# A gate stage as one hand-ordered stream over rows of 8x8 blocks, in a four-layer convolution and scan kernel

## The chip, the cores and the metric

The kernel runs on one core of one Trainium2 chip. The metric is the device time of one execution in microseconds; where several executions are compared, their median is given. All arithmetic is float32.

## The reference, cut to what matters

An image batch x of shape (2, 128, 128, 128) (two images, 128 channels, 128 by 128 pixels) goes through four layers. Layers 0 and 2 are a 3x3 convolution, a small selective scan (mamba) of 8 tokens per pixel, a group norm, a SiLU and a residual. Layer 3 is a residual block of two 3x3 convolutions with batch norm. Layer 1, which the change concerns, weighs x with a gate made from local densities:

```python
g = x.reshape(B, GROUP, c, hh, WINDOW, ww, WINDOW)      # 4 groups of 32 channels, 16 x 16 windows of 8 x 8
g = g.transpose(0, 1, 3, 5, 2, 4, 6).reshape(B * GROUP * hh * ww, c, WINDOW * WINDOW)
sq = jnp.sum(g * g, axis=-1)
gram = jnp.einsum('ncw,ndw->ncd', g, g)
dist2 = jnp.maximum(sq[:, :, None] + sq[:, None, :] - 2.0 * gram, 0.0)
K = jnp.exp(-0.5 * dist2 / (BW * BW))
density = K.mean(axis=-1)                                # one number per channel and window
y = jnp.einsum('bchw,oc->bohw', density, w1) + b1[None, :, None, None]
y = jax.nn.relu(y)
y = jnp.einsum('bchw,oc->bohw', y, w2) + b2[None, :, None, None]
attn = jax.nn.sigmoid(y) + GAMMA                         # GAMMA = 0.5
attn = upsample_bilinear_ac(attn, WINDOW)                # 16 x 16 -> 128 x 128, corners aligned
return x * attn
```

The norm, SiLU and residual of layer 0 need statistics over a whole image, so the kernel computes them in the gate stage too, just ahead of the densities.

## The kernel before, in words

The program runs in five parts, one after another: mamba layer 0 (`_mamba`, lines 296 to 580), the gate stage (`_gates`, 602 to 775), mamba layer 2 (the same function again), the norms, and the residual block (`_basic_block`). Each part opens its own buffer pools and closes them at its end, so a part's first buffers come free when the part before has let go of that memory. A tile framework gives out buffers and sets every semaphore. It also lets two engines touch the same PSUM bank only one after the other, even when both only read. Within `_mamba` the order of each engine's instructions is written out by hand (`tc.manual_schedule`, line 577). In `_gates` of the kernel before it is not: there the framework's scheduler orders each engine's queue by the order of the program text and by what is ready.

Work in `_gates` goes by rows of windows: a row is (b, y0), image b and one of 16 rows of 8x8 windows, 8 pixel rows high, so 128 channels by 1024 pixels. There are 32 rows. For each row:

- `load` (629) brings the mamba output (tile g) and the layer's input (tile xr) from memory, 512 KB each; ScalarE applies the norm and SiLU to g (636), GpSimd adds xr and stores the sum by windows in a tile x (638).
- `turn` (646) transposes x in eight pieces of 128x128 on TensorE into a PSUM tile pt (652). VectorE copies pt out as xt (654) and ScalarE squares it into xq (656). ScalarE also squares x itself into sq (659), VectorE sums that for each window (661) and scales the sums by -0.5 (662): nsq.
- `density` (665) makes the Gram matrices on TensorE: 8 matmuls with the constant -0.5 (671) and 64 of 32x32 (681), in eight tiles of the array side by side. VectorE adds nsq out of PSUM (689, tile kk), GpSimd clips at 0 (695), ScalarE takes the Exp (696).
- `total` (699) sums kk over channels on VectorE into dens (700).

When the 16 rows of an image have their densities, `gain` (702) computes the gates of the whole image: one matmul with w1, a Relu, and for each of four groups of windows two matmuls (717, 718), a Sigmoid (719) and an addition of 0.5 (720). From then on `apply` (722) is called once in each step of the loop: it upsamples one row of the gates on TensorE (738), in matmuls that contract 32 partitions (two neighbouring gate rows), and multiplies it into x on VectorE (747), in one to two pieces a row; ScalarE's queue issues the store (751). So the loop (756 to 773) runs image 0's densities alone, then image 1's densities with image 0's upsampling, and the last line (775) runs image 1's upsampling alone. All 16 rows of an image wait in SBUF for their gates (tile x has nh + 5 = 21 buffers). Large PSUM tiles (pt, the upsampled rows, the gates) share one tag with two buffers of three banks.

ScalarE's functions come in tables: Silu has one, Exp another, Sigmoid a third, and an instruction that changes the table (a table load) stands in ScalarE's queue wherever the next function needs another one. Square and Relu need no change.

Of the kernel before, what the change touches and what calls it, by code (L numbers as in the profile page):

```python
# [24 lines left out]
F32 = mybir.dt.float32  # L25
U8 = mybir.dt.uint8
AF = mybir.ActivationFunctionType
ALU = mybir.AluOpType
AX = mybir.AxisListType
PSUM = bass.MemoryType.PSUM  # L30

P = 128
# [7 lines left out]
WIN = 8  # L40
# [37 lines left out]
def _bilinear(n):  # L78

    m = n // WIN  # L80
    at = np.arange(n, dtype=np.float32) * np.float32((m - 1) / (n - 1))
    i0 = np.clip(np.floor(at).astype(np.int32), 0, m - 2)
    return i0, (at - i0.astype(np.float32)).astype(np.float32)
# [8 lines left out]
def _place(k):  # L92


    q = k // 2
    return k % 2 + 2 * (q // 4), q % 4


def _upsampling(H):

    _, fy = _bilinear(H)
    ix, fx = _bilinear(P)
    wx = np.zeros((P // WIN, P), np.float32)
    wx[ix, np.arange(P)] = 1.0 - fx
    wx[ix + 1, np.arange(P)] += fx
    segs = _segments(H)
    up = np.zeros((4, 2, P // WIN, 4, max(e - a for _, a, e in segs), P), np.float32)
    for k, a, e in segs:
        n, g = _place(k)
        for h in range(a, e):  # L110
            up[g, 0, :, n, h - a] = (1.0 - fy[h]) * wx
            up[g, 1, :, n, h - a] = fy[h] * wx
    return up.reshape(P, 4, -1)
# [488 lines left out]
def _gates(tc, src, w, con, y, stats, wm, b1, up, dst, H):  # L602

    nc = tc.nc
# [3 lines left out]
    nwin = nh * nw  # L608
    segs = _segments(H)
    with tc.tile_pool(name="dg", bufs=2) as dp, tc.tile_pool(name="dg1", bufs=1) as sp, tc.tile_pool(  # L610
        name="ps_t", bufs=2, space=PSUM
    ) as pst, tc.tile_pool(name="ps_g", bufs=1, space=PSUM) as psg:

        def wide():
            return pst.tile([P, 3 * ROWS, P], F32, tag="pt", name="pt")

        class Small:


            def tile(self, shape, dtype, tag=None, name=None):  # L620
                return wide().rearrange("p a b -> p (a b)")[: shape[0], : shape[1]]

        norm = [_norm(nc, sp, Small(), w, con, stats, b) for b in range(B)]
        ct = sp.tile([P, 4, up.shape[2]], F32, tag="ct", name="ct")

        dens = [sp.tile([P, nh, 2, npair], F32, tag=f"dens{b}", name="dens") for b in range(B)]
        held, live, gains = {}, {}, {}

        def load(b, y0):

            rows = slice(y0 * WIN, (y0 + 1) * WIN)
            g = dp.tile([P, WIN, P], F32, tag="g", name="g", bufs=4)
            nc.sync.dma_start(out=g, in_=y[b][:, rows, :])
            xr = dp.tile([P, WIN, P], F32, tag="xr", name="xr", bufs=4)
            nc.sync.dma_start(out=xr, in_=src[b][:, rows, :])
            nc.scalar.activation(g, g, AF.Silu, bias=norm[b][1], scale=norm[b][0])
            x = held[b, y0] = dp.tile([P, nw, WIN, WIN], F32, tag="x1", name="x1", bufs=nh + 5)
            nc.gpsimd.tensor_tensor(by_row(x), by_row(xr, False), by_row(g, False), ALU.add)
# [6 lines left out]

        def turn(b, y0):

            x = held[b, y0].rearrange("p x r w -> p (x r w)")

            pt = wide()[:, :npair, :]  # L650
            for k in range(npair):
                nc.tensor.transpose(pt[:, k, :], x[:, k * P : (k + 1) * P], con["ident"])
            xt = dp.tile([P, npair, P], F32, tag="xt", name="xt")
            nc.vector.tensor_copy(xt, pt)
            xq = dp.tile([P, npair, P], F32, tag="xq", name="xq")
            nc.scalar.activation(xq, pt, AF.Square)

            sq = dp.tile([P, nw, WIN * WIN], F32, tag="sq", name="sq", bufs=1)
            nc.scalar.activation(sq.rearrange("p x r -> p (x r)"), x, AF.Square)
            nsq = dp.tile([P, nw], F32, tag="nsq", name="nsq")  # L660
            nc.vector.tensor_reduce(nsq, sq, AX.X, ALU.add)
            nc.vector.tensor_scalar_mul(nsq, nsq, -0.5)
            live[b, y0] = xt, xq, nsq

        def density(b, y0):
            xt, xq, nsq = live.pop((b, y0))
# [21 lines left out]
            kk = dp.tile([P, 2, npair, CG], F32, tag="kk", name="kk", bufs=3)  # L688
# [8 lines left out]
            live[b, y0] = kk  # L697

        def total(b, y0):
            nc.vector.tensor_reduce(dens[b][:, y0], live.pop((b, y0)), AX.X, ALU.add)  # L700

        def gain(b):

            den = sp.tile([P, nh, npair, 2], F32, tag="den", name="den")
            nc.vector.tensor_scalar_mul(den, dens[b].rearrange("p y a k -> p y k a"), 1.0 / CG)
            p1 = wide().rearrange("p a b -> p (a b)")[:CG, :nwin]
            nc.tensor.matmul(p1, lhsT=wm["w1"], rhs=den.rearrange("p y k a -> p (y k a)"), start=True, stop=True)
            hid = sp.tile([CG, nwin], F32, tag="hid", name="hid")
            nc.scalar.activation(hid, p1, AF.Relu, bias=b1)
            p2 = wide()[:, :4, :]  # L710
            gt = gains[b] = sp.tile([P, 4, P], F32, tag="gain", name="gain")
            for n in range(4):
                at = (n % 2 + n // 2 * WIN) * nw
                m = min(P, nwin - at) // 32 * 32
                if m <= 0:
                    continue
                nc.tensor.matmul(p2[:m, n, :], lhsT=hid[:, at : at + m], rhs=wm["w2"], start=True, stop=False)
                nc.tensor.matmul(p2[:m, n, :], lhsT=wm["one"][:, :m], rhs=wm["b2"], start=False, stop=True)
                nc.scalar.activation(gt[:m, n, :], p2[:m, n, :], AF.Sigmoid)
                nc.vector.tensor_scalar_add(gt[:m, n, :], gt[:m, n, :], 0.5)  # L720

        def apply(b, y0):

            r0 = y0 * WIN
            pu = wide()
            o = dp.tile([P, WIN, P], F32, tag="g", name="o", bufs=4)
            x = by_row(held.pop((b, y0)))

            cut = [a for k, a, _ in segs if k % 2 == 0 and r0 < a < r0 + WIN]
            at = 0  # L730
            for first, end in zip([r0, *cut], [*cut, r0 + WIN]):
                for r in range(first, end, ROWS):
                    for k, a, e in segs:
                        lo, hi = max(a, r), min(e, r + ROWS, end)
                        if lo < hi:
                            n, g = _place(k)
                            q = slice(g * 32, (g + 1) * 32)
                            nc.tensor.matmul(
                                pu[:, at + lo - first : at + hi - first, :],
                                lhsT=gains[b][q, n, :],  # L740
                                rhs=ct[q, n, (lo - a) * P : (hi - a) * P],
                                start=True,
                                stop=True,
                                tile_position=(q.start, 0),
                            )
                rows = slice(first - r0, end - r0)
                nc.vector.tensor_tensor(
                    by_row(o[:, rows, :], False), by_row(pu[:, at : at + end - first, :], False), x[:, rows], ALU.mult
                )
                at += (end - first + ROWS - 1) // ROWS * ROWS  # L750
            nc.scalar.dma_start(out=dst[b][:, r0 : r0 + WIN, :], in_=o)

        order = [(b, y0) for b in range(B) for y0 in range(nh)]
        N = len(order)
        ready = []
        for n in range(-4, N + 2):
            if ready:
                apply(*ready.pop(0))
            if n % 2 == 0:
                for i in range(n + 4, min(n + 6, N)):  # L760
                    load(*order[i])
            if n == -4:
                nc.sync.dma_start(out=ct, in_=up)
            if 0 <= n < N:
                turn(*order[n])
            if 1 <= n <= N:
                density(*order[n - 1])
            if n >= 2:
                b, y0 = order[n - 2]
                total(b, y0)  # L770
                if y0 == nh - 1:
                    gain(b)
                    ready += [(b, i) for i in range(nh)]
        for at in ready:
            apply(*at)
# [141 lines left out]
def _program(ctx, tc, d, cols, out):  # L917
# [7 lines left out]
    with tc.tile_pool(name="const", bufs=1) as cp, tc.tile_pool(name="wts", bufs=1) as wp:  # L925
# [6 lines left out]
        w2 = cp.tile([CG, 3, P], F32, tag="w2", name="w2")  # L932
# [3 lines left out]
        wm = {"w1": w1, "w2": w2[:, 0, :], "b2": w2[:, 1, :], "one": w2[:, 2, :]}  # L936
# [18 lines left out]
def _host_layout(inputs):  # L955
# [9 lines left out]
    w2b = np.zeros((CG, 3, P), np.float32)  # L965
    w2b[:, 0] = np.asarray(inputs["L1_conv_w2"]).T
    w2b[0, 1] = np.asarray(inputs["L1_conv_b2"])
    w2b[:, 2] = 1.0
# [27 lines left out]
```

## Time and profile before

| | |
|---|---|
| time, median of 3 executions | 7872.17 us (7866.06 to 7881.12) |
| profiled execution | 7862.75 us; span of the core 7860.9 us |
| granted TensorE clock, mean over the span | 0.923 of full |
| busy share of the span | PE 83%, DVE 87%, ACT 55%, POOL 70% |
| last multiply of the gate stage (L747) ends | about 3633.6 us from the start |
| first load of the next layer's rows can start | 3638.4 us |

The profile's short names are: PE for TensorE's matmuls and PEld for its weight loads, DVE for VectorE, ACT for ScalarE, POOL for GpSimd, SP for the queue that issues most transfers. L652 is line 652 of the kernel. In the tables of stretches, each engine's busy time in microseconds stands with its number of instructions in brackets; after the engines come the granted clock, the busy share of the transfer engines and GB/s. In the timeline, each line is a start and a duration in microseconds, engine, line, operation, and tiles (out<-in); what stands in square brackets at the end is the idle time of the engine before the instruction, and what ended it.

A float32 matmul shows as two records on TensorE, a transpose as one.

### The profile page before, as it was taken

How to read it: one execution, taken by the hardware profiler on the slowest of the kernel's cores; microseconds unless marked ns; L12 is line 12 of the kernel's file. 1: busy time of each engine (PE TensorE's matmuls, PEld its weight loads, DVE VectorE, ACT ScalarE, POOL GpSimd, SP SyncE). 2: the span in 40 equal slices, each digit the busy share in tenths (PEclk: the TensorE clock that was granted, in tenths of full speed). 3: DMA queues.
4: the chain of work that ended last, by engine and by line, in shares of the span. 5: the costliest groups of instructions: out<-in, count | busy, mean ns of one | idle time of the engine just before them, and what ended most of it. 6: DMA issues, size and time to landing. Idle time of an engine off the chain costs nothing. (4 is left out here: it accounts for less than half of the span.)

```text
span 7860.9 us, 86792 instructions
## 1 busy us (share of the span) xinstructions
PE 6537.9 (83%) x29412; PEld 2217.4 (28%) x29412; DVE 6831.1 (87%) x6360; ACT 4291.8 (55%) x4835; POOL 5521.1 (70%) x1810
## 2 busy tenths in 40 slices
PE   7888888888888888777888888888888888878893
PEld 2222222222222222253222222222222222223341
DVE  5999999999999999863999999999999999963454
ACT  5656666666666656482665665666656656621112
POOL 5777887777778777652777778787777777843330
PEclk8999999999999999866999999999999999979996
DMA  7999999999999999854999999999999999955204
GB/s 203 246 243 246 253 249 247 253 250 256 249 248 254 245 249 248 225 179 127 244 249 246 250 250 251 252 251 253 252 239 249 250 250 250 250 157 139 69 0 163
DMA packets 573435, 1765.42 MB, mean 225 GB/s; under 512 B 85536, under 2 KB 239680, under 8 KB 458176
## 3 DMA queue, kind: packets, MB, share of 16 engines
q1 hardware_dynamic: 530496, 1709.54, 84.0%
q10 hardware_dynamic: 42496, 50.34, 1.8%
q8 instruction: 234, 3.83, 0.2%
q14 instruction: 209, 1.71, 0.1%
HBM read 1549.82 MB, written 209.72 MB: 224 GB/s over the span
## 5 line engine op out<-in xcount | busy, mean ns | idle before, releaser
L451 POOL TENSOR_TENSOR h<-ur,bcr 128x2048 f32<-128x2048 f32 x896 | 4060.4, 4539 | 1193.2 <-DMA bcr<-sb 1006.0
L478 DVE TENSOR_TENSOR set<-set,h 128x1024 f32<-128x1024 f32 x1792 | 2193.0, 1224 | 301.6 <-ACT set L469 216.2
L479 DVE TENSOR_TENSOR r<-set,bcr 128x1024 f32<-128x1024 f32 x1792 | 2194.1, 1224 | 61.4
L469 ACT ACTIVATE set<-set 128x1024 f32<-128x1024 f32 x1792 | 1745.6, 1006 | 868.7 <-PE set L460 854.2
L483 DVE TENSOR_TENSOR h<-set,h 128x1024 f32<-128x1024 f32 x1536 | 1864.5, 1214 | 21.3 <-POOL h L451 21.2
L460 PE MATMUL set<-dt,rep 32*128 32x512 f32 x7168 | 1400.2, 674 | 96.8 <-DVE h L483 89.9
L498 PE MATMUL ys<-r,ct 128*32 128x512 f32 x7168 | 1166.1, 632 | 36.4 <-DVE r L479 36.0
L328 PE MATMUL one<-band,conv 128*128 128x512 f32 x2304 | 1085.5, 607 | 24.6 <-DMA band<-in_x_dram 12.2
L828 PE MATMUL m<-comb,u 128*128 128x512 f32 x1536 | 689.1, 610 | 88.5 <-DVE Y L842 53.2
L406 PE MATMUL one<-xc,keep 128*64 128x512 f32 x1024 | 324.6, 717 | 471.4 <-ACT xc L363 361.5
L460 PEld LDWEIGHTS set<-dt,rep 32*128 32x128 f32 x7168 | 405.2, 193 | 992.7 <-issue 466.2
L328 PEld LDWEIGHTS one<-band,conv 128*128 128x128 f32 x2304 | 408.2, 190 | 674.4 <-issue 599.2
L489 PE MATMUL ys<-t,ct 128*128 128x512 f32 x512 | 326.4, 724 | 252.4 <-DVE v L511 250.9
L357 ACT ACTIVATE xc<-one,keep 128x512 f32<-128x512 f32 x256 | 176.1, 688 | 519.5 <-PE one L355 514.7
L498 PEld LDWEIGHTS ys<-r,ct 128*32 128x32 f32 x7168 | 181.2, 111 | 928.5 <-issue 760.7
L828 PEld LDWEIGHTS m<-comb,u 128*128 128x128 f32 x1536 | 296.6, 195 | 480.3 <-issue 457.3
L426 PE MATMUL one<-prod,ct 128*128 128x512 f32 x512 | 290.3, 650 | 123.1 <-POOL prod L418 88.8
L380 POOL TENSOR_TENSOR u<-dt,xc 128x1024 f32<-128x1024 f32 x128 | 302.8, 2366 | 70.7 <-ACT dt L374 70.6
L355 PE MATMUL one<-y,w_in 128*128 128x512 f32 x512 | 343.5, 759 | 5.8 <-ACT xc L357 3.1
L469 ACT ACT_TABLE_LOAD x252 | 323.3, 1283 | 4.6
L370 PE MATMUL one<-xc,w_dt 128*128 128x512 f32 x512 | 313.5, 696 | 4.1 <-ACT bc L413 4.1
L427 ACT COPY t<-one 128x512 f32<-128x512 f32 x256 | 150.2, 587 | 301.4 <-PE one L426 301.4
(136 smaller groups left out, 5894.0 us busy)
## 6 DMA issues: line engine op xcount, KB each, us to landing
ur<-su SPq DMA_DIRECT2D x896, 896.0 KB, 11.5
bcr<-sb SPq DMA_DIRECT2D x896, 448.0 KB, 11.6
ur<-su SPq DMA_DIRECT2D x896, 128.0 KB, 11.1
su<-u SPq DMA_DIRECT2D x1024, 64.0 KB, 3.5
sb<-bc SPq DMA_DIRECT2D x256, 224.0 KB, 2.8
bcr<-sb SPq DMA_DIRECT2D x896, 64.0 KB, 10.9
y<-o SPq DMA_DIRECT2D x128, 256.0 KB, 9.2
band<-in_x_dram SPq DMA_DIRECT2D x28, 640.0 KB, 10.9
```

The source lines that it names most:

```text
L328: nc.tensor.matmul(py.rearrange("p (r w) -> p r w", r=ROWS), lhsT=w["conv"][:, tap, :], rhs=xb[:, r + kh : r + kh + ROWS, kw : kw + P], st ...
L355: nc.tensor.matmul(p, lhsT=w[("in", "z")[i]][:, g, :], rhs=s["y"], start=True, stop=True)
L406: nc.tensor.matmul(p[g * NQ * DS : (g + 1) * NQ * DS, :], lhsT=w[("xb", "xcm")[i]], rhs=s["xc"][:, g, :], start=True, stop=True,)
L451: nc.gpsimd.tensor_tensor(b, s["ur", t], s["bc", t][:, 0].unsqueeze(1).to_broadcast([P, NJ, NS]), ALU.mult)
L460: nc.tensor.matmul(a[j // 2][:, j % 2, :], lhsT=w["rep"][r, q, :], rhs=s["dt"][r, g, :], start=True, stop=True, tile_position=(r.start, 0),)
L469: nc.scalar.activation(x, x, AF.Exp)
L478: nc.vector.tensor_tensor(pt, pt, s["h", t - 1][:, js, :], ALU.mult)
L479: nc.vector.tensor_tensor(s["r", t][:, js, :], pt, s["bc", t - 1][:, 1].unsqueeze(1).to_broadcast([P, 2, NS]), ALU.mult)
L483: nc.vector.tensor_tensor(s["h", t][:, js, :], pt, s["h", t][:, js, :], ALU.add)
L489: nc.tensor.matmul(s["ys", g], lhsT=con["ident"], rhs=s["t1"][:, g, :], start=True, stop=False)
L498: nc.tensor.matmul(s["ys", g][a : a + NQ * DJ, :], lhsT=red[:, q, :], rhs=r[:, j, :], start=False, stop=(q == NQ - 1), tile_position=(0, a),)
L828: nc.tensor.matmul(m[:, i], lhsT=u[:, i, kw, :], rhs=v[:, i, :, kw : kw + P], start=(kw == 0), stop=(kw == 2),)
```

## The change

The stage becomes one stream over all 32 rows. Each row's gate is made as soon as the densities of its neighbours are there, instead of once for an image, and is used five to seven steps after the row's densities were begun. So a row of x waits for its gate in one of 14 buffers instead of 21, the upsampling of both images runs beside densities, and the order of every engine's queue is written out: step n of the loop runs the stages of rows n, n-1, n-2, n-3, n-5, n-6 and n-7, in the order in which the list `stages` has them. The Sigmoid is computed as 1 / (1 + exp(-y)), with ScalarE's Exp and a reciprocal on VectorE, so the stage needs two tables, and rows are loaded and their Silu is applied in pairs, on even steps. The upsampling contracts 64 partitions (four gate rows, of which the weights use up to three), with two matmuls of 512 columns for each row of windows. The stores are issued from SP's queue.

The diff, cut to its core:

```diff
+    up = np.zeros((2, 4, P // WIN, H // WIN, ROWS, P), np.float32)
+    for h in range(H):
+        y0, r = divmod(h, WIN)
+        for y, f in ((iy[h], 1.0 - fy[h]), (iy[h] + 1, fy[h])):
+            if f != 0:
+                up[r // ROWS, y - y0 + 1, :, y0, r % ROWS] = f * wx
...
-        def wide():
-            return pst.tile([P, 3 * ROWS, P], F32, tag="pt", name="pt")
...
+        weights = sp.tile([P, nh, ROWS * P], F32, tag="up", name="up")
+        nc.sync.dma_start(out=weights.rearrange("p y n -> p (y n)"), in_=up)
+        hidden = []
+        for b in range(B):
+            h = sp.tile([CG, nh + 3, nw], F32, tag=f"hid{b}", name="hid")
+            nc.gpsimd.memset(h, 0.0)
+            hidden.append(h)
...
+        def residual(b, y0):
+            s = live[b, y0]
+            g, xr = s.pop("g"), s.pop("xr")
+            nc.scalar.activation(g, g, AF.Silu, bias=norm[b][1], scale=norm[b][0])
+            s["x"] = dp.tile([P, nw, WIN, WIN], F32, tag="x1", name="x1", bufs=14)
+            nc.gpsimd.tensor_tensor(by_row(s["x"]), by_row(xr, False), by_row(g, False), ALU.add)
...
         def turn(b, y0):
-            pt = wide()[:, :npair, :]
+            pt = pst.tile([P, npair, P], F32, tag="pt", name="pt")
...
-        def gain(b):
-            den = sp.tile([P, nh, npair, 2], F32, tag="den", name="den")
...
-                nc.scalar.activation(gt[:m, n, :], p2[:m, n, :], AF.Sigmoid)
-                nc.vector.tensor_scalar_add(gt[:m, n, :], gt[:m, n, :], 0.5)
+        def hide(b, y0):
+            p = psg.tile([CG, nw], F32, tag="one", name="ph")
+            nc.tensor.matmul(
+                p, lhsT=wm["w1"], rhs=live[b, y0].pop("den").rearrange("p a k -> p k a"), start=True, stop=True
+            )
+            nc.scalar.activation(hidden[b][:, y0 + 1, :], p, AF.Relu, bias=b1, scale=1.0 / CG)
+
+        def gate(b, y0):
+            s = live[b, y0]
+            p = psg.tile([P, P], F32, tag="one", name="pz")
+            h = hidden[b][:, y0 : y0 + 4, :].rearrange("p y x -> p (y x)")
+            for a in range(0, P, P // 2):
+                nc.tensor.matmul(p[a : a + P // 2, :], lhsT=h, rhs=wm["w2"], start=True, stop=False)
+                nc.tensor.matmul(p[a : a + P // 2, :], lhsT=wm["one"], rhs=wm["b2"], start=False, stop=True)
+            s["e"] = dp.tile([P, P], F32, tag="e", name="e")
+            nc.scalar.activation(s["e"], p, AF.Exp, scale=-1.0)
+
+        def gain(b, y0):
+            e = live[b, y0]["e"]
+            nc.vector.tensor_scalar_add(e, e, 1.0)
+            nc.vector.reciprocal(e, e)
+            nc.vector.tensor_scalar_add(e, e, 0.5)
+
+        def spread(b, y0):
+            s = live[b, y0]
+            pu = s["pu"] = pst.tile([P, 2 * ROWS, P], F32, tag="pt", name="pu")
+            for n in range(2):
+                q = slice(n * P // 2, (n + 1) * P // 2)
+                nc.tensor.matmul(
+                    pu[:, n * ROWS : (n + 1) * ROWS, :].rearrange("p r w -> p (r w)"),
+                    lhsT=s["e"][q, :],
+                    rhs=weights[q, y0, :],
+                    start=True,
+                    stop=True,
+                )
+
         def apply(b, y0):
...
+            o = s["o"] = dp.tile([P, WIN, P], F32, tag="o", name="o")
+            nc.vector.tensor_tensor(by_row(o, False), by_row(s["pu"], False), by_row(s["x"]), ALU.mult)
+
+        def keep(b, y0):
+            nc.sync.dma_start(out=dst[b][:, y0 * WIN : (y0 + 1) * WIN, :], in_=live.pop((b, y0))["o"])
...
-        for n in range(-4, N + 2):
-            if ready:
-                apply(*ready.pop(0))
...
+        stages = ((0, turn), (1, density), (2, total), (3, hide), (5, gate), (6, gain), (6, spread), (7, apply), (7, keep))
+        E = mybir.EngineType
+        with tc.manual_schedule(engines={E.PE, E.Activation, E.DVE, E.Pool, E.SP}):
+            for n in range(-6, N + 8):
+                if n % 2 == 0:
+                    for m in range(max(n + 4, 0), min(n + 6, N)):
+                        load(*order[m])
+                    for m in range(max(n + 2, 0), min(n + 4, N)):
+                        residual(*order[m])
+                for lag, stage in stages:
+                    if 0 <= n - lag < N:
+                        stage(*order[n - lag])
```

## The prediction

> **What bounds the kernel now.** The table of slices comes first: the whole kernel is two long, nearly identical stretches (the two mamba layers, VectorE at 9) with a dip in slices 16 to 18, and a tail. The change lies in the dip.
>
> ```profile
> PE   7888888888888888777888888888888888878893
> DVE  5999999999999999863999999999999999963454
> ACT  5656666666666656482665665666656656621112
> POOL 5777887777778777652777778787777777843330
> PEclk8999999999999999866999999999999999979996
> ```
>
> Cutting the dip by what runs in it gives the stage's three parts, from 3337 to 3638 us (the numbers after the stretch are its length, then busy us of PE, weight loads, DVE, ACT and POOL, the granted clock, DMA):
>
> ```profile
> 3337.00:3450.00 113.00, 67.42 (x2596) 53.56 (x2596) 69.48 (x87) 108.45 (x104) 72.31 (x38) 0.71 0.61 207
> 3450.00:3571.00 121.00, 105.46 (x2375) 67.08 (x2374) 80.19 (x102) 66.92 (x72) 48.24 (x26) 0.68 0.37 133
> 3571.00:3638.00 67.00, 58.51 (x106) 29.31 (x106) 21.42 (x28) 2.85 (x6) 0.00 (x0) 0.50 0.33 133
> ```
>
> Image 0's densities: ScalarE is 96% busy and bounds them, 113/16 = 7.1 us a row. Image 1's densities with image 0's upsampling: TensorE carries it, 121/16 = 7.6 us a row. Then image 1's upsampling alone, 67/16 = 4.2 us a row, on TensorE at clock 0.50. In all 301 us for 32 rows, 9.4 us a row: the change has to beat this mean. DMA is at 0.61 at most.
>
> The timeline of one row then shows how a density hands over from engine to engine (start, duration, engine, line):
>
> ```profile
> 3440.90 1.21 DVE L654 COPY xt<-pt 128x1024 f32<-128x1024 f32 x1
> ...
> 3442.73 1.00 ACT L656 ACTIVATE xq<-pt 128x1024 f32<-128x1024 f32 x1
> 3443.63 1.04 ACT L659 ACTIVATE sq<-x 128x1024 f32<-128x1024 f32 x1
> ...
> 3444.71 1.22 DVE L661 TENSOR_REDUCE nsq<-sq 128x16 f32<-128x1024 f32 x1 [2.59 <-ACT sq L659]
> ...
> 3447.25 0.68 DVE L689 TENSOR_TENSOR kk<-pg,nsq 128x512 f32<-128x512 f32 x1
> ...
> 3448.02 1.49 POOL L695 TENSOR_SCALAR kk<-kk 128x512 f32<-128x512 f32 x1 [5.80 <-DVE kk L689]
> ...
> 3449.54 0.63 ACT L696 ACTIVATE kk<-kk 128x512 f32<-128x512 f32 x1 [1.06 <-POOL kk L695]
> ```
>
> Each follows its producer by 0.03 to 0.09 us. Eight transposes on TensorE take 1.97 or 1.09 us, by the clock of the moment:
>
> ```profile
> 3469.07 1.97 PE L652 MATMUL pt<-ct,x 128*128 128x128 f32 x8 [1.39 <-DVE o L747]
> ...
> 3473.75 1.09 PE L652 MATMUL pt<-ct,x 128*128 128x128 f32 x8
> ```
>
> **What the Trainium skill says.** "TensorE: Matmul & The Clock Gate", Part 1: the array runs at half clock by default and after an idle window of about 3.4 us, and at full clock after about as long busy. The trace shows both rates (1.97 against 1.09), but in the last stretch 58.5 us busy of 67 did not lift the clock from 0.50: matmuls with 32 rows do not warm it here. "ScalarE: Activation LUTs", What ACT_TABLE_LOAD costs: 1283 ns a load, which L636 and L696 show exactly; about 280 ns plus 0.833 per element for an activation with a bias operand, near what L709 shows (465 ns for 256 elements). "VectorE: DVE Perf Modes", the walkthrough of the pipeline, says reciprocal repeats a divide step 8 times; no long reciprocal is in the trace. "TensorEngine Tiling (Array Packing)", Key Properties: tiles in different row or column groups run in parallel; L460 agrees (8 records in four row groups in 1.18 us, where one 512-column record costs 0.43).
>
> **The change part by part.**
> - Table loads: gone are 46 loads (21 + 22 + 3); the new order has 15 of Silu and 15 of Exp. 16 x 1.283 = 20.5 us of ScalarE saved. It bounded only the first stretch, and does not bound the new loop below.
> - Upsampling: 88 matmuls of 32 rows (176 records; L738 keeps TensorE busy for 44.6 us of the second stretch and 53.7 of the third) become 64 of 64 rows, two a row. Multiplies (L747): 46 become 32. The gate of a whole image (L705 to L720) becomes, for each row, one small matmul, a Relu, four matmuls of 128 columns, an Exp and three VectorE operations. The extra VectorE work is 32 x (0.22 + R + 0.22), where 0.22 is L720; R, the 128x128 reciprocal, lies between 0.22 and 128 x 8 / 0.96 GHz = 1.07 plus 0.15. I take 1.2; the row still has idle VectorE time behind it, so R is off the path either way.
> - The third stretch of 67 us, upsampling alone, goes: the last rows need only the drain worked out below.
> - The upsampling table grows from 4608 to 8192 floats a partition. L763's 2304 KB landed in 8.8 us, so 4096 KB take an estimated 15.6 us, ahead of the first loads on the same queue: they start about 4 us later. ScalarE also has four Silus ahead of the first square now, the fourth waiting for its load. First square: 3340.9 before, about 3347 after.
> - Weights prefetch, both mamba layers and the last layer keep their order: nothing.
>
> **The new wait.** The hand order fixes each engine's queue, and within step n it ties the engines in a ring. TensorE: transposes(n), density(n-1), hide(n-3), gate(n-5), spread(n-6). ScalarE: on even steps two Silus; then xq(n), sq(n), Exp of kk(n-1), Relu(n-3), Exp(n-5). VectorE: xt(n), nsq(n), kk(n-1), total(n-2), gain(n-6), apply(n-7). The gate of row n-5 reads the hidden row n-3, so it waits for the Relu of this same step; the Relu stands behind Exp of kk(n-1), which waits for GpSimd's min, which waits for VectorE's kk(n-1), which stands behind nsq(n), which waits for sq(n), which stands behind xq(n), which waits for xt(n), which waits for transposes(n). And transposes(n+1) stand behind gate and spread on TensorE. So one turn of the ring is one row:
>
> xt 0.23 + 1.22; xq 0.03 + 0.91 (start to start); sq 1.05 + 0.03; nsq 1.22 + 0.03; scaling and kk 0.09 + 0.69 + 0.09; min 1.49 + 0.03; Exp 0.53 (start to start); Relu on 16 columns 0.27; to TensorE 0.04. Sum **7.95 us** without TensorE.
>
> TensorE's part: the four gate matmuls, eight records. L717 with L718, four records, took 0.98 to 1.22 us at half clock, so 1.1 if the two column groups overlap and 2.2 if not; I take 1.5. Spread, two 512-column matmuls in two row groups: one took 1.91 us at half clock (L738), so 2.0 if they overlap and 3.6 if not; I take 2.0. Transposes 1.0 to 2.0; I take 1.6. Sum 5.1 at the half clock I expect, since TensorE idles some 5 us of each turn, waiting for the Relu. At full clock 0.7 + 1.1 + 1.0 = 2.8.
>
> **A turn is 13.0 us**, against 9.4 us a row now. Hidden in it: density (2.3 us behind the transposes, needed 4.6 us after xt starts), total, gain and apply (VectorE has 3 to 4 us to spare), GpSimd's two additions of 2.36, and the Silus of even steps (from the gate's end 0.2 + 0.28 + 1.28 + 2.37 = 4.1 us, when xq comes 5.1 after it).
>
> Steps 0 to 4 have no gate. Their ring is 6.3 us on odd steps; even ones add a load and two Silus, 3.65. From the first square at 3347 to the Relu of step 5 I get 44 us: 3391. Then 26 turns of 13.0 = 338: 3729. Then the drain: density(31) to Relu 9, three rows of hide, gate and spread at about 4, three of gate and spread at about 3, the last apply: 31 us, so 3760. The last multiply ended at 3633.6 before. Difference +126 us; the storing and the next layer's start follow as before. 7872 + 126 = **7998 us**.
>
> **The rivals.**
> 1. Work alone decides (faster). The ring binds less than I think, and the busiest engine sets the pace: TensorE at half clock 2.0 + 2.3 + 0.3 + 1.5 + 2.0 = 8.1 us a row, 259 for 32, plus 30 for fill and drain: 289 from 3347 gives 3636; with VectorE's 6.9 as the pace and a warm array, 251 and 3598. That is 0 to -36 us, say 7850. For it: engines were busy at once in stretch 2. Against it: every link of the ring is a fixed place in a queue or a data dependence.
> 2. The ring with a warm array: 7.95 + 2.8 + 0.2 (even steps then wait for their Silus) = 10.9 us. 26 x 2.1 = 55 less and 5 in the drain: 7938. For it: 1.09 us transposes occur at 70% clock. Against it: the idle time in each turn.
> 3. The ring with no overlap in gate and spread: 7.95 + 2.2 + 3.6 + 2.0 = 15.7 us; 26 x 2.7 = 70 more and 4 in the drain: 8072. For it: L738's matmuls ran one after another, though on the same row group. Against it: L460.
>
> **How the numbers follow.** The ring at half clock 0.52, warm 0.22, without overlap 0.16; work alone 0.06; something that cancels out, within 0.2% of before, 0.04. The range takes in rivals 2 and 3 and leaves out rival 1 and no change, 0.10: 7930 to 8075. Faster 0.06, same 0.03, slower 0.91.
>
> **What would show it.** Right: VectorE's wait of nsq for sq about 2 us in every row; TensorE's gate matmuls waiting some 5 us a row for the Relu; rows about 13 us apart; the stage's clock at 0.5 to 0.65; ScalarE well under 60% in the stage; the stage some 420 us from first square to last multiply. Wrong: rows under 9.4 us apart, or gate matmuls that do not wait.

## The result, and the profile after

| | before | after |
|---|---|---|
| median time | 7876.65 us (7866.06 to 7887.21, 4 runs) | 7991.97 us (7988.0 to 7999.94, 4 runs) |
| ratio to before | | 1.0148 (95% interval 1.0130 to 1.0165) |
| stage, from the issue of the upsampling table's load to the first clearing of the next layer's band | 321.97 us | 436.73 us |
| rest of the kernel behind the stage | 4222.5 us | 4216.4 us |

The changed kernel is 115.3 us slower in the medians. In the two profiled executions the stage alone is 114.8 us longer; of the rest, the part ahead of the stage is 16.7 us longer and the part behind it 6.1 us shorter. The change leaves that code as it was, and differences of this size occur without it: in the ten profiles of this document the stage begins between 3310.5 and 3333.1 us. So the loss lies in the stage. The forecast was 7998, or 126 us more. It looks nearer in the total than it is in the difference because the fourth execution of before raised that kernel's median by 4.5 us.

The slices of the changed kernel's page, the same rows as were shown of before:

```profile
PE   7888888888888888655888888888888888878893
DVE  5999999999999999744799999999999999963454
ACT  4656665665666666443556666666666666621112
POOL 5777777887777787531687787787777777844330
PEclk8999999999999999766999999999999999979996
```

The 18th digit of each row is a slice that lies wholly in the stage, in both kernels. It was PE 7, DVE 6, ACT 8, POOL 5; now it is 5, 4, 4 and 3. Every engine is less busy than before, and none is near 9. The stretch of the steady loop says the same in microseconds (the stretch, its length, then busy us of PE, weight loads, DVE, ACT and POOL, the granted clock, DMA):

```profile
3395.00:3730.00 335.00, 186.66 (x4312) 120.76 (x4312) 162.20 (x232) 138.72 (x180) 96.64 (x52) 0.66 0.30 108
```

TensorE is 56% busy, VectorE 48%, ScalarE 41%, DMA 30%. Before, some engine was at 87 to 96% in each of the three parts. When all engines are half idle and the list of waits shows none for DMA, the time is most likely in a chain that runs from engine to engine. The list of waits for the same stretch names the links (the waiting instruction, what it waited for, us in total, how many times, the longest):

```profile
POOL kk L689 <- DVE kk L683: 172.6, 27, 11.4
...
PE pz L711 <- ACT hid L703: 143.2, 26, 6.2
DVE xt L648 <- PE pt L646: 109.0, 25, 5.5
...
DVE nsq L655 <- ACT sq L653: 55.6, 26, 2.8
```

TensorE's gate matmuls (L711) wait for the Relu (L703) 26 times, 5.5 us each; nsq waits 2.1 us for sq, 26 times. The timeline of one turn, from the gate's matmul to the next gate's matmul, shows the chain itself. Each line starts shortly after the one before it has ended or, within one engine's queue, as the next to run; where the engine had been idle, the brackets name what ended that:

```profile
3571.57 0.70 PE L711 MATMUL pz<-w,hid 32*64 32x128 f32 x4 [5.43 <-ACT hid L703]
...
3572.62 2.08 PE L729 MATMUL pu<-up,e 64*128 64x512 f32 x4
...
3574.63 1.97 PE L646 MATMUL pt<-ct,x 128*128 128x128 f32 x8
...
3576.63 1.23 DVE L648 COPY xt<-pt 128x1024 f32<-128x1024 f32 x1 [4.35 <-PE pt L646]
...
3577.95 1.02 ACT L650 ACTIVATE xq<-pt 128x1024 f32<-128x1024 f32 x1 [4.93 <-DVE xt L648]
3578.87 1.05 ACT L653 ACTIVATE sq<-x 128x1024 f32<-128x1024 f32 x1
...
3579.95 1.22 DVE L655 TENSOR_REDUCE nsq<-sq 128x16 f32<-128x1024 f32 x1 [2.10 <-ACT sq L653]
...
3581.29 0.68 DVE L683 TENSOR_TENSOR kk<-pg,nsq 128x512 f32<-128x512 f32 x1
...
3582.06 1.49 POOL L689 TENSOR_SCALAR kk<-kk 128x512 f32<-128x512 f32 x1 [11.36 <-DVE kk L683]
...
3583.58 0.63 ACT L690 ACTIVATE kk<-kk 128x512 f32<-128x512 f32 x1 [3.66 <-POOL kk L689]
...
3584.11 0.25 ACT L703 ACTIVATE hid<-ph,b 32x16 f32<-32x16 f32 x1
...
3584.42 0.69 PE L711 MATMUL pz<-w,hid 32*64 32x128 f32 x4 [5.30 <-ACT hid L703]
```

In three of four turns of the steady loop a row takes 12.85 us, as here; in the fourth the transposes are some 0.2 us shorter. The mean distance of the xt copies from 3440 to 3700 is 12.80. Before, the mean over the stage was 9.4.

### The profile page after: what moved, and what is told of

It reads as the page before. It is cut to its first block, busy times and chain, and to the rows that moved or that the text cites. A ratio compares the mean times of both kernels' runs of the same rounds, so it can differ in the third digit from the quotient of the medians.

```text
span 7986.2 us, 87413 instructions
## 1 busy us (share of the span) xinstructions
PE 6553.9 (82%) x29648; PEld 2221.8 (28%) x29648; DVE 6865.4 (86%) x6432; ACT 4285.3 (54%) x4873; POOL 5522.1 (69%) x1812
## 5 line engine op out<-in xcount | busy, mean ns | idle before, releaser
L426 POOL TENSOR_TENSOR t<-t,xc 128x1024 f32<-128x1024 f32 x128 | 302.3, 2362 | 10.0
## 6 DMA issues: line engine op xcount, KB each, us to landing
band<-in_x_dram SPq DMA_DIRECT2D x28, 640.0 KB, 10.9
```

## The experiments

Two theories were set against each other: that the hand order closes a **ring** through all four engines, so that one turn of it is one row; and that the **stream itself** costs the time (the added work on VectorE, the clock, TensorE's amount of work). All but e7 and e5 change one thing in the changed kernel; "a row" is the mean distance of the xt copies from 3440 to 3700 unless another stretch is named. Each ratio is to the kernel before, run beside it on the same chip.

**e1: the gate one row later.**

```diff
-        stages = (..., (3, hide), (5, gate), (6, gain), (6, spread), (7, apply), (7, keep))
+        stages = (..., (3, hide), (6, gate), (7, gain), (7, spread), (8, apply), (8, keep))
```

> The changed kernel with gate, gain, spread and apply one step later (lags 6, 7, 7, 8 for 5, 6, 6, 7); the same work. Ring theory: the gate matmuls no longer wait for the Relu of their own step, so the ring that goes through GpSimd's clip, the Exp and the Relu opens. The next ring closes through gain, which stands behind kk(n-1) and total(n-2) on VectorE: xt to kk 5.2 us, total 0.6, gain 1.45, spread 2.0, transposes 2.0 and 0.1 of handing over: 11.4 us a row for 12.84. 26 rows by 1.4 is 37 less, one more step of drain gives 3 back: about 7958 us (1.010 of before). Rival, the work itself sets the pace (TensorE at half clock, more VectorE work): the same work in the same engines, so 7992 and 12.8 us a row as now.

Measured: 7992.57 us, ratio 1.0145 (1.0118 to 1.0172), 12.79 us a row. The expectation missed: nothing moved. The waits of this kernel, from 3420 to 3600, give the reason:

```profile
PE pz L711 <- ACT hid L703: 78.9, 14, 5.9
```

The gate of row n-6 needs a hidden row that was written a step ago, and yet it waits for the Relu of this step, 5.6 us each time. What it waits for can't be that row's data. The lines of the two tiles show what else there is: `ph` (L699) and `pz` (L708) have the same tag in a PSUM pool with one buffer, so pz can be written only when the Relu has read ph. A data edge and a buffer edge lay on top of each other, and the prediction had seen only the first. The next two kernels take them apart.

**e8: pz in a buffer of its own, at the old distance.**

```diff
-            p = psg.tile([P, P], F32, tag="one", name="pz")
+            p = psg.tile([P, P], F32, tag="gate", name="pz")
```

> After with one edit: pz in a PSUM buffer of its own, the distances of after. Theory: the gate of row n-5 reads hid of row n-3, which the Relu of the same step writes, so the data wait closes the same ring with or without the shared buffer: 12.84 us a row, 7992 (7985 to 7999), L711 still waits some 5.4 us for L703. Rival (the buffer alone closes the ring): 11.4 us a row, 7958.

Measured: 7978.81 us, ratio 1.0151 (1.0134 to 1.0168), 12.66 us a row, and the same wait:

```profile
PE pz L711 <- ACT hid L703: 67.0, 12, 5.9
```

The data edge alone holds the ring closed too.

**e7: both, the gate one row later and a buffer of its own.**

> As e1 (gate six rows behind the turn, gain and spread seven, apply and keep eight), and the gate's product pz gets a PSUM buffer of its own in place of the one it shared with ph. Theory: in e1 the data of the gate was ready a step earlier, and its matmuls L711 waited for the Relu L703 only because that Relu frees the one buffer. With both cut, the ring closes a shorter way: T, xt, xq, sq, nsq, kk, total (0.68), gain (0.27 + 0.95 + 0.23), spread (2.08), next T (1.97). From the timeline of after, the start of xt to the end of gain is 7.4 us without the wait on GpSimd; with spread and T 11.4 us a row instead of 12.85, so about 35 us less: 7958, and L711 waits for the Relu no more. Rival (it is the distance of one step that counts, or the half clock of TensorE, and the buffer is no matter): 12.85 us a row and 7992 as in e1.

Measured: 7939.51 us, ratio 1.0108 (1.0082 to 1.0135), 11.45 us a row. The wait for the Relu is gone from TensorE's matmuls of the gate, and another has come, the one that was forecast:

```profile
PE pu L729 <- DVE e L721: 67.0, 16, 5.1
```

The spread now waits 4.2 us a row for the gain, which stands on VectorE behind kk and the row sums of this step. So of the four combinations, three are at 12.7 to 12.8 us a row and only the one without either edge is at 11.45. The stage is 40.3 us shorter than in after, where about 35 had been expected. The ring was closed twice, and behind it lay a second, shorter one.

**e2: shorten a link.** GpSimd's min (1.49 us), a link of the ring, goes to VectorE.

```diff
-            nc.gpsimd.tensor_scalar_min(kk, kk, 0.0)
+            nc.vector.tensor_scalar_min(kk, kk, 0.0)
```

> The changed kernel with the clip at 0 of each row's kk on VectorE instead of GpSimd. Ring theory: the clip is a link of the ring; 1.49 us and two handings-over (0.12) become about 0.45 on VectorE, so a row takes 11.7 us for 12.84: 26 by 1.15 is 30 less, about 7962 us, though GpSimd was busy less than a third of the stage and VectorE gets 14 us of work more. Rival, the work sets the pace and GpSimd has time to spare: no gain, or VectorE's 14 us more: 7992 to 8006.

Measured: 7950.02 us, ratio 1.0098 (1.0076 to 1.0121), 11.95 us a row. The timeline of this kernel, same links as above:

```profile
3560.60 0.68 DVE L683 TENSOR_TENSOR kk<-pg,nsq 128x512 f32<-128x512 f32 x1
3561.32 0.43 DVE L689 TENSOR_SCALAR kk<-kk 128x512 f32<-128x512 f32 x1
...
3561.78 0.63 ACT L690 ACTIVATE kk<-kk 128x512 f32<-128x512 f32 x1 [1.25 <-DVE kk L689]
```

From kk's start to the Exp it is 1.18 us instead of 2.29. VectorE has more work, and the row is shorter by 0.85 us. From the start of xt to the gate a turn now takes 6.67 us instead of 7.78, the whole 1.11 that the link gave up. Some 0.2 of it is lost again between gate and spread (1.25 us instead of 1.05), and the transposes have hardly any short turns left. What counts is the link's latency, not the load of the engine.

**e3: lengthen work beside the ring.** A useless copy of 1.22 us a row on VectorE, ahead of each multiply.

```diff
             o = s["o"] = dp.tile([P, WIN, P], F32, tag="o", name="o")
+            nc.vector.tensor_copy(o, s["pu"])
             nc.vector.tensor_tensor(by_row(o, False), by_row(s["pu"], False), by_row(s["x"]), ALU.mult)
```

> The changed kernel with one useless VectorE copy of a 128x1024 tile more in each row (the upsampled gates are copied to o just before the multiply overwrites o): 32 by 1.22 = 39 us of VectorE work. Ring theory: it lies in VectorE's idle time behind gain, off the ring: 12.84 us a row as now, two or three us more in the drain: 7994 us. Rival, VectorE's added work is what the change costs: 39 us more, 8031.

Measured: 7975.9 us, ratio 1.0130 (1.0109 to 1.0150), 12.80 us a row. In its timeline the copy eats only idle time: xt's wait for the transposes shrinks from 4.35 to 3.02 us.

```profile
3485.62 1.22 DVE L740 COPY o<-pu 128x1024 f32<-128x1024 f32 x1
3486.94 1.23 DVE L741 TENSOR_TENSOR o<-pu,x 128x1024 f32<-128x1024 f32 x1
3491.18 1.23 DVE L648 COPY xt<-pt 128x1024 f32<-128x1024 f32 x1 [3.02 <-PE pt L646]
```

1.22 us in 32 rows is 39 us of work, and the stage grew by 5.7, from 436.7 to 442.5. With e2 it makes a pair: what lies on the ring counts, and what lies beside it hardly does.

**e6: does more work on TensorE lift the clock?** Two useless matmuls a row, into a buffer that nothing reads, in the time in which TensorE waits for the Relu.

```diff
+            fill = psg.tile([P, 4 * P], F32, tag="fill", name="fill")
+            for _ in range(2):
+                nc.tensor.matmul(fill, lhsT=con["ident"], rhs=weights[:, 0, :], start=True, stop=True)
```

> After with two useless 128x128x512 matmuls a row on TensorE behind the matmul of hide, into a PSUM buffer that nothing reads, where TensorE waits 5.4 us a row for the Relu. At the half clock they take about 2 us (from L646: 1024 columns in 1.97 us), so they fit into the wait. Theory A (ring; TensorE's part of it, gate 1.05 + spread 2.0 + T 2.0, is slow because the clock stays at half, and more activity lifts it): up to 2.2 us a row less, some 7935 at best. Theory B (ring, and this much work does not move the clock): 12.84 us a row, 7992. Rival (TensorE's amount of work sets the row): 2 us a row more, 8044.

Measured: 7984.51 us, ratio 1.0158 (1.0142 to 1.0175), 12.56 us a row, within 0.3 us of theory B. Theory A's 10.6 us a row did not come, nor the rival's 2 us more. But theory B's reason, that this much work doesn't move the clock, isn't what happened. The timeline of TensorE tells more than the time:

```profile
3556.97 1.11 PE L665 MATMUL pg<-xq,ct 64*32 64x256 f32 x16
...
3559.35 1.98 PE L706 MATMUL fill<-up,ct 128*128 128x512 f32 x4
3564.86 0.56 PE L714 MATMUL pz<-w,hid 32*64 32x128 f32 x4 [3.52 <-ACT hid L703]
...
3565.78 2.08 PE L732 MATMUL pu<-up,e 64*128 64x512 f32 x4
3567.79 1.97 PE L646 MATMUL pt<-ct,x 128*128 128x128 f32 x8
```

The mean granted clock from 3420 to 3720 went from 0.67 to 0.77, but it is the fillers that ran fast. A float32 matmul is two records (the expectation had counted one), so the two fillers are 2048 columns in 1.98 us, where the transposes' 1024 take 1.97. After them TensorE still waits 3.5 us, and spread and transposes, the part that lies on the ring, run at the slow rate as before in most rows (transposes at 1.96 or 1.97 us in 20 of 24, spread at 2.08 in 19). In 10 of 23 turns the gate, the spread or the transposes ran faster, and these rows took 11.7 to 12.7 us; the part from xt to the gate stayed at 7.78 us in all. This is theory A in a small part, and the stage is 8.0 us shorter than in after. The Trainium skill, "TensorE: Matmul & The Clock Gate", Part 1, has the rate follow windows of about 3.4 us of idle or busy time. What is seen is compatible with that: in the row shown, spread and transposes fall into the first 4.9 us behind the wait (3564.86 to 3569.76), and the faster rate comes only behind them. That these windows set it is not shown; it was not tried further. A higher mean clock of a stage is hardly a gain where the fast time falls beside the path.

**e4: the same stream, ordered by the scheduler.** `with tc.manual_schedule(...)` is left out of the stage; nothing else changes.

> The changed kernel with the same stages, buffers and lags, but without the hand order in the gate stage: the framework's scheduler orders the queues, as in the kernel before. Ring theory: the order alone closes the ring; a scheduler that puts an instruction that is ready ahead of one that waits opens it, and rows take about 8 to 10 us: 26 rows by 3 to 5 less, 7860 to 7910 us. Rival, the stream itself (a gate for each row, smaller matmuls, a table that is larger) is what costs: 7980 to 8000 whatever the order.

Measured: 7854.12 us, ratio 0.9981 (0.9970 to 0.9992), 8.58 us a row from 3400 to 3600, stage 312.7 us. The wait of the gate for the Relu, from 3420 to 3600, has shrunk to almost nothing:

```profile
PE pz L711 <- ACT hid L703: 4.2, 7, 0.9
```

It is even below the expected 7860 to 7910. The stage is 124 us shorter than with the hand order, with the same operations and buffers. So the stream is no slower than the stage of before, and even a little faster; the written order is what costs.

**e5: a hand order without the ring.** The order of a step is rewritten so that hardly anything waits for something issued in the same step:

```diff
-        stages = ((0, turn), (1, density), (2, total), (3, hide), (5, gate), (6, gain), (6, spread), (7, apply), (7, keep))
+        first = ((7, gain), (8, apply), (8, keep), (0, square), (2, soft), (3, hide), (6, gate))
+        then = ((0, turn), (0, norms), (1, density), (2, total), (7, spread))
...
-                for lag, stage in stages:
+                for lag, stage in first + then:
...
+                if n % 2 == 0:
+                    for m in range(max(n + 2, 0), min(n + 4, N)):
+                        residual(*order[m])
```

`square` is sq, now ahead of the transposes and xq; `norms` is nsq; `soft` is the Exp, a step after GpSimd's min; pz has its own buffer; the Silus come at the end of a step.

> The same operations on the same data, still one hand-ordered stream, with the order inside a step rewritten so that no operation waits for one issued in the same step: gain, apply and keep of rows n-7 and n-8 first, then the square of row n ahead of its transposes on ScalarE, the Exp one step after GpSimd's min, hide, the gate at n-6 with a PSUM buffer of its own, then the transposes of n, norms, density, total, spread, and the silu and residual at the end of the step. Theory (in-order queues closed a ring; the work itself is much shorter): a row costs what the busiest engine does in it, TensorE at the half clock 7.6 us (gate 1.05, spread 2.0, T 2.0, density 2.0, hide 0.24), VectorE 6.6: 7.6 to 7.9 us a row, stage 285 to 305 us, 7830 to 7865. Rival (the stream itself, with its bursts and half clock, is the cost and a hand order can do no better than the scheduler): about e4's 7854 or above, up to 7992.

Measured: 7834.8 us, ratio 0.9958 (0.9940 to 0.9975), 7.53 us a row from 3420 to 3579, stage 285.3 us. The time and the stage lie in the expected ranges and the row just under its range (7.6 to 7.9), but the engine that was to set the pace isn't the one that does, as the stretch below suggests. This beats the kernel before by 0.4% and, by the two ratios, each against before (0.9958 / 1.0148), the changed kernel by 1.9%. Its stretch from 3420 to 3600:

```profile
3420.00:3600.00 180.00, 140.87 (x3843) 93.02 (x3842) 162.93 (x218) 113.83 (x156) 81.01 (x43) 0.78 0.49 178
```

VectorE is busy for 162.9 of 180 us, 91%, TensorE for 78%, and the clock is 0.78. So an engine is nearly full again, but it is VectorE, and not TensorE at the half clock with its 7.6 us a row. The shortest rows are 6.2 us, the longest 10.9.

## Why the prediction was right

The forecast was 126 us more; measured were 115.3 in the medians and 114.8 in the stage. Step by step:

- **The ring.** Forecast 13.0 us a row, measured 12.85 in the turn shown (3571.57 to 3584.42, start of L711 to start of L711). Its terms: gate 1.05 (1.5 taken between 1.1 and 2.2), so the two column groups overlap nearly fully, as "TensorEngine Tiling (Array Packing)", Key Properties, has it; spread 2.01 (2.0 taken between 2.0 and 3.6), so the two row groups overlap too; transposes to the start of xt 2.00 (1.6 + 0.23), as they run at the slow rate in 18 of 24 turns; from xt to the gate 7.79 (7.72). The first term was too long by 0.45 and the third too short by 0.17, so that the sum is in part better than its terms. Rival 3 (no overlap) is refuted by the first two, rival 2 (warm array) by the transposes.
- **The edge that closes it.** Right as far as it went: the gate waits for the Relu of the same step. That a shared PSUM buffer closes the same ring a second time was missed; it cost nothing here, but by the reasoning of the prediction e1 would have opened the ring, and it did not.
- **Start, turns, drain.** The timeline of after holds the four marks, the first square, the Relu of step 5, the Relu of step 31 and the last multiply:

```profile
3360.72 1.00 ACT L650 ACTIVATE xq<-pt 128x1024 f32<-128x1024 f32 x1
...
3405.73 0.25 ACT L703 ACTIVATE hid<-ph,b 32x16 f32<-32x16 f32 x1
...
3737.79 0.25 ACT L703 ACTIVATE hid<-ph,b 32x16 f32<-32x16 f32 x1
...
3765.52 1.23 DVE L740 TENSOR_TENSOR o<-pu,x 128x1024 f32<-128x1024 f32 x1 [0.82 <-PE pu L729]
```

  Fill 45.0 us (44), 26 turns 332.1 (338), drain 29.0 (31); together 406.0, where the prediction's own marks give 413 (its closing "some 420" was loose). Before, the same span was 292.7. The first square of a transposed row (xq), counted from the start of the stage, comes 3.1 us later than before (forecast 6), and the next layer begins 1.7 us sooner behind the last multiply. 113.3 + 3.1 - 1.7 is 114.8 with unrounded terms. The some 11 us too many are, rounded, 6 of the turns, 2 of the drain, 3 of the start and 1.7 of the end, less 1 of the fill. In the profiled run of after, the layer ahead ended later, and the table's load was issued at 3333.06 instead of 3316.4; this load's issue is therefore the zero in both.
- **VectorE's reciprocal.** Taken as 1.2 us, an estimate by the upper bound worked out from "VectorE: DVE Perf Modes", the walkthrough of the pipeline; measured 0.95. In this order it lies off the path, as the copy of e3 does at nearly the same place; in e7, where spread waits for gain, it lies on it.
- **What would show it.** nsq's wait about 2 us (2.1), the gate's about 5 (5.5), rows about 13 us apart (12.8), ScalarE well under 60% (41%): as written. The clock, forecast at 0.5 to 0.65, was 0.66, just above.
- **A reading that was too wide.** "Each follows its producer by 0.03 to 0.09 us" holds for nsq, GpSimd's min and the Exp in the lines given for it. There xq begins 0.62 us after xt's end and kk 1.1 us after the scaling of nsq, because ScalarE and VectorE did work of other rows first. In the ring of after the short gaps are there for xq too (3577.95, where xt ends at 3577.86), so the sum was not hurt.
- **Rival 1** (work alone decides, 7850) did not happen in the changed kernel. For the same stream without the ring its numbers were of the right size: 8.1 us a row for TensorE at the half clock and 6.9 for VectorE, against 8.58 in e4 and 7.53 in e5, where VectorE is the fullest engine.

What stays open: e4 and e5 also run at a higher granted clock (0.77 and 0.78 from 3420 to 3600). By the prediction's estimate for TensorE's part of the ring, 5.1 us at half clock and 2.8 at full, this can give some 2.3 us a row at most, of the 4.2 and 5.3 us that they gain; how much of that it gave was not tried. Beyond that, e4 and e5 change many places in the queues at once, so which of their moves is worth how much beyond the two edges of e7 and the link of e2 was not tried. Nor was the worth of the single parts of the change in e4, the saved table loads and the wider upsampling. That matmuls of 32 rows are what kept the clock at 0.50 in the last stretch of before is a reading that no run tests.

## What to carry to other kernels

Before a software pipeline is ordered by hand, write down each engine's queue for one step and follow what each instruction waits for, through data, through the order of its queue and through buffers with few copies; if the walk comes back to its start one step on, the sum of the latencies on it is the time of a step, however idle the engines are. In the profile such a ring looks like this: no engine near full, the same few waits once in every row with nearly the same length, and a constant distance of rows. To open it, move consumers a step behind their producers and give their tiles buffers of their own; here either alone changed next to nothing (12.79 and 12.66 us a row), and both together uncovered the next ring (11.45). Only when the rings are gone does the load of an engine begin to count again, as VectorE's 91% in e5.

## What was not expected of the hardware

- The granted clock of a stage says little on the rate of the matmuls that matter: with fillers (e6) it rose from 0.67 to 0.77, and the transposes on the path stayed at 1.96 or 1.97 us in 20 of 24 rows, where 1.09 is the fast rate.
- Matmuls of one row of windows in two row groups overlap fully even with 512 columns each: both took 2.08 us at the slow rate, where one alone, of 32 rows, had taken 1.91 before. The prediction had left this open between 2.0 and 3.6.
- A float32 reciprocal of 128x128 took 0.95 us on VectorE, against 0.23 to 0.27 for an addition of a constant on the same tile.
